# Layer 0 of a two-layer graph network: neighbours summed before the weights are applied, one tile of zeros for two fills, and moved register loads and stores in layer 1

## The chip, the cores and the metric

The kernel runs on one core of a Trainium2 chip. The metric is device microseconds (us) of one execution, taken as the median of several runs. One execution was also recorded by the hardware profiler; all rows below come from that one. Engines are named as in the profile: PE (matrix products; PEld is its weight load), DVE (vector), ACT (scalar and activation functions), POOL, SP (issues most transfers). A small q behind a name (SPq) is the engine's own instruction queue.

## The reference, cut to what matters

Two layers of the same kind, on 3327 tokens of 256 features. Each is a graph step and then a mixture of experts, both added to x:

```python
# layer 0
x = x + relu(adj @ (_layernorm(x) @ W) + b)                      # graph step
xn = _layernorm(x)
gate_scores = xn @ Wg.T + bg                                     # 8 experts, best 2
x = x + sum_e combine[:, e] * (relu(xn @ W1[e].T + b1[e]) @ W2[e].T + b2[e])   # hidden 1024
# layer 1
xn = _layernorm(x)
h2 = tanh(xn @ W_proj + b_proj)
x = x + relu(top700(tanh(adj * adj)) @ (h2 @ W_gcn) + b_gcn)
xn = _layernorm(x)
x = x + xn + sum_e combine[:, e] * (gelu(xn @ w1[e] + b1[e]) @ w2[e] + b2[e])  # hidden 256
```

The layer norm has no learnt scale or shift. `adj` is 3327 x 3327 in float32, with about one entry in 400 set. A row of it keeps its largest 700 entries in layer 1, which changes nothing while no row has more.

## The kernel before

Tokens are padded to 26 tiles of 128 (`NT`). `x` and `s` hold all tiles on the chip, 128 tokens on the partitions and 256 features along a row. The adjacency comes transposed from memory in 13 panels (`NPAN`) of 256 output tokens; a panel is two pieces (`NCHUNK`) of 13 source tiles (`CJ`), 1664 KB each, and lies in a ring of six buffers (`RING`), so three panels fit.

**Layer 0, features (L1021 to L1037).** For the 26 tiles in groups of 2, 2, 4, 4, 6 and 8, DVE works out mean and deviation (`statistics`, L254 to L279, with three Newton steps for the root). PE turns each raw tile by two 128x128 transposes (L304), ACT copies two turned tiles at once (L305), PE multiplies by the weights (`node_features`, L312), and ACT scales the result by the deviation into `s` (L317). The mean is taken out of the weights once, by a product with a tile of 1/256 (L1030, L1033). 32 small matmuls (`WARM`, L144) run on PE ahead of all this.

**Layer 0, panels (`aggregate`, L348 to L367).** For each panel PE sums over the 26 source tiles, for each of its two output tiles in turn: the weights of the array are 128x128 of the adjacency, the moving operand is a row of `s` (L358). DVE adds bias and relu onto `x` (L322, L323), then `after0` normalises the two finished tiles, takes 16 score products (L378, with `gate`, the expert gates spread over all partitions) and ranks them. The tokens of panel p are written to their experts' lists in memory one panel later (`list_tokens`): PE needs the ranks (`rt_both`, L415) for counting them (L464, L465), POOL issues the scatters (L482). ACT counts the set entries of each piece (`count`, L1046, 16 activations a panel) to see that no row exceeds 700; ACT also takes the exponential of the weights (L443), which DVE waits for (L445).

**Fill and gates.** Behind the panel loads `after0(0)` has SP transpose both layers' gates into memory, element by element (L1062, 2048 elements each), has POOL load the first one spread over partitions (L247), and calls `fill`: for each expert's list a tile of zeros with row numbers in one column is made by POOL (L1009, L1010) and stored by SP (L1013), 8 in `after0(0)` and 8 in `after0(1)`. The tiles come from a pool of two.

**Experts.** A step handles one block of up to 256 listed tokens of one expert: `first` (turned block times w1, L865, function on ACT, L872), the transposes of the next block (L853), `second` (L904, bias and weight on DVE, L911, L912, then scatter to `ys`). Blocks are loaded five ahead into the ring by SP: list rows (L820), w1 (L827), b1 (L831), and for some w2 and b2. In layer 1 all of w2 and b2 is on the chip.

**Layer 1, end.** `plan` works out on the chip which blocks exist; a flag says whether the counts are as usual, and both engines branch (L1297). Inside, `know` reads the experts of the last columns into registers of PE and DVE (L789), since those of the first 16 are known numbers. There are 32 steps. From the 17th on, pairs of finished token tiles are read back from `ys` (L968), added to `x` by DVE two steps later (L982), and stored by SP another step later (L1304); the last pairs follow in `finish` (L1266).

Every engine works through its own instruction list in order. The lists are made when the program is built, by priorities and dependencies; an instruction that waits holds up all behind it on its engine, and on SP and POOL the transfers behind it. SP's transfers take eight semaphores in turn, so that one is issued when the transfer eight places before it has landed.

Of the kernel before, what the change touches and what calls it, by code (L numbers as in the profile page):

```python
# [22 lines left out]
P = 128  # L23
NT = 26
# [52 lines left out]

BEGUN, FIRST_TILES, MORE_TILES = 12, 14, 22
WARM = 32
# [11 lines left out]
def gnn_moe_two_layers(  # L91
# [39 lines left out]

    proj_sb = const.tile([P, DC, D], F32, name="proj_sb")
    for t, n in [(0, 2)] + [(t, 4) for t in range(2, NT, 4)]:
        nc.sync.dma_start(out=x[:, t : t + n, :], in_=x_in[:, t : t + n, :])
        if t == 0:
            nc.sync.dma_start(out=proj_sb, in_=g0_w.rearrange("(c p) n -> p c n", p=P))
# [10 lines left out]
    mean = ring[RING - 1][:, 0:P]  # L147
    nc.gpsimd.memset(mean, 1.0 / D)
# [95 lines left out]
    gates = []  # L244

# [6 lines left out]
    g1_bp_sb = plain("g1_bp_sb", g1_bp)  # L252
    g1_wg_sb = by_feature("g1_wg_sb", g1_wg)
# [54 lines left out]
    def node_features(i, lhsT, w_sb, scale=None):  # L308

        ps = psy.tile([P, D], F32, name="ps_s", tag="py")  # L310
        for c in range(DC):
            nc.tensor.matmul(  # L312
                ps, lhsT=lhsT[:, c, :], rhs=w_sb[:, c, :], start=(c == 0), stop=(c == DC - 1)
            )
        if scale is None:
            return nc.scalar.copy(s[:, i, :], ps)
        return nc.scalar.activation(s[:, i, :], ps, AF.Copy, scale=scale)  # L317
# [12 lines left out]
    def piece(pan, k):  # L330
        return ring[(pan * NCHUNK + k) % RING].rearrange("p (c w) -> p c w", w=PW)

    last_piece, output_loads = [], []

    def load_panel(pan, prepare, earlier=()):

        for k in range(NCHUNK):
# [6 lines left out]
    def aggregate(b_sb, prepare, after, loaded=0, count=None):  # L344

        for pan in range(NPAN):
# [4 lines left out]
            if count:  # L351
                count(pan, chunks)
# [14 lines left out]
            after(pan)  # L367

# [383 lines left out]
    def experts(xlist, ys, group, fixed, n_hidden, func, w1T, b1, w2T, b2, copy, kept=None):  # L752
# [5 lines left out]
        own_n, all_w2, all_b2 = kept or (EARLY + LATE, None, None)  # L758
# [18 lines left out]
        def expert(t, late, engines):  # L777

            table, col = late[0] if t >= EARLY else early_table, col_of(t)
            if known and t >= EARLY:  # L780
                if col < known[0]:
                    return col % E
                if engines != [SP]:
                    return known[1][col - known[0]]
            return nc.values_load(table[0:1, 0, col : col + 1], engines=engines, min_val=0, max_val=E - 1)

        def know(n, late):

            _, registers = nc.values_load_multi_w_load_instructions(  # L789
                late[0][0:1, 0, n : LATE_PAIRS + fixed], engines=[PE, DVE], min_val=0, max_val=E - 1  # L790
            )
            known[:] = [n, registers]
# [12 lines left out]
        def load_one(late):  # L805
# [21 lines left out]
            nc.sync.dma_start(  # L827
                out=w1, in_=w1T[ds(e, 1), :, :].rearrange("o (c p) h -> p (o c) h", p=P)
            )
            bb1 = view("b1")  # L830
# [89 lines left out]

        always = EARLY + LATE_PAIRS + fixed

        def step(late, end=always, place=None):
# [8 lines left out]
            hT = first(ready.pop(t), w1, bb1, groups_of(t))  # L932
            if t + 1 < min(len(loaded), end):
# [21 lines left out]
        def back_to(old):  # L955
# [8 lines left out]
            state=state, back_to=back_to, know=know, tiers_done=tiers_done(), always=always,  # L964
# [38 lines left out]
    def fill(xlist):  # L1003

        with tc.issue_after(last_feature.ins):
            for e in range(E):
                zeros = blk.tile([P, H // P, SB], F32, name="wide").rearrange("p h b -> p (h b)")
                zeros = zeros[:, 0 : SG * RW].rearrange("p (g d) -> p g d", g=SG)
                nc.gpsimd.memset(zeros, 0.0)  # L1009
                nc.gpsimd.tensor_scalar(  # L1010
                    zeros[:, :, ID], slot, float(AWAY + SPARE + (LATE + e) * SB), None, ALU.add
                )
                nc.sync.dma_start(  # L1013
                    out=xlist[e * NP : e * NP + SB, :].rearrange("(g p) d -> p g d", p=P),
                    in_=zeros,
                )

    deviation = {}  # L1021
    for t0, n0 in [(0, 2), (2, 2), (4, 4), (8, 4), (12, 6), (18, 8)]:
        _, rs = statistics(t0, n0)
        deviation.update((t0 + g, rs[:, g : g + 1]) for g in range(n0))
        for t in range(t0, t0 + n0, 2):
            xT = turned_tiles([x[:, t + g, :] for g in range(2)])
            if t == 0:
                ps = psy.tile([P, D], F32, name="ps_mean", tag="py")
                for c in range(DC):
                    nc.tensor.matmul(  # L1030
                        ps, lhsT=mean, rhs=proj_sb[:, c, :], start=(c == 0), stop=(c == DC - 1)
                    )
                nc.vector.tensor_tensor(  # L1033
                    proj_sb, proj_sb, ps.unsqueeze(1).to_broadcast([P, DC, D]), ALU.subtract
                )
            for g in range(2):
                last_feature = node_features(  # L1037
                    t + g, xT[:, :, ts(g, P)], proj_sb, deviation[t + g]
                )

    def count(pan, chunks):
        with tc.issue_after(last_feature.ins):
            for k, a in enumerate(chunks):
                for i in range(PW // GROUP):
                    sign = work.tile([P, CJ, GROUP], BF16, name="sign", bufs=1)
                    nc.scalar.activation(  # L1046
                        sign, a[:, :, ts(i, GROUP)], AF.Sign, bias=below,
# [446 lines left out]
```

## Time and profile before

| | |
|---|---|
| median of 3 runs | 1244.86 us (1243.46 to 1245.89) |
| profiled execution, its own time | 1245.38 us |
| its span | 1243.6 us |
| instructions | 18251 |
| PE busy | 1202.0 us, 97% of the span |
| DVE / ACT / POOL busy | 698.0 / 522.5 / 280.9 us |
| moved | 241.60 MB, mean 194 GB/s |
| layer 0: first matmul of the panels, last of them | 44.30 us, 344.87 us |
| layer 1: last matmul of the panels | 1094.86 us |
| last matmul of all | 1226.25 us |

The span is what the records cover; 1.8 us of the execution's own time lie around it. In the lists of waits the columns are: engine, the instruction's output tile and line, what released it, then the sum of the idle time in us, how often, and the longest. In a timeline they are: start in us, duration in us, engine, line, operation, output and inputs, shape, count, and in brackets the idle time before it and what ended it. A matmul of float32 on 128x128 with 256 columns shows as two records.

### The profile page before, as it was taken

The numbers are of one execution on the slowest core, as the hardware profiler recorded it, in microseconds if no ns is written. First come the engines' busy times: TensorE is split into PE (matmuls) and PEld (weight loads), VectorE is DVE, ScalarE is ACT, GpSimd is POOL, SyncE is SP. The second block draws the span as 40 slices with busy tenths as digits, with TensorE's granted clock in tenths as the row PEclk, the third lists the DMA queues.
The fourth block names the chain that finished last, engine by engine and source line by source line (L and its number), as shares of the span: only waits on it lengthen the run. The fifth ranks groups of instructions, "written<-read, shape, count | busy, mean of one in ns | idle before, by whom it ended". The sixth has DMA issues, their size and how long they took to land. (4 is left out here: it accounts for less than half of the span.)

```text
span 1243.6 us, 18251 instructions
## 1 busy us (share of the span) xinstructions
PE 1202.0 (97%) x5853; PEld 1040.3 (84%) x5853; DVE 698.0 (56%) x2812; ACT 522.5 (42%) x963; POOL 280.9 (23%) x367
## 2 busy tenths in 40 slices
PE   7999899999999999999999999999999999999993
PEld 6888788888888888888888888888888888877882
DVE  5064967768755111211111166658999998875464
ACT  4785654551022222222232235895555453043331
POOL 2022313112122111111111110002422323254441
PEclk9999899999999999999999999999999999999997
DMA  9568445544266567575757676344554442476697
GB/s 346 169 194 279 158 169 200 179 146 155 98 215 208 181 197 237 178 230 180 232 173 242 209 273 237 110 149 152 192 182 167 166 176 85 122 247 206 200 296 236
DMA packets 119738, 241.60 MB, mean 194 GB/s; under 512 B 21568, under 2 KB 90192, under 8 KB 112592
## 3 DMA queue, kind: packets, MB, share of 16 engines
q1 hardware_dynamic: 107984, 208.23, 50.2%
q0 software_dynamic: 11104, 31.59, 7.0%
q8 instruction: 48, 0.79, 0.3%
q14 instruction: 58, 0.48, 0.1%
q10 hardware_dynamic: 544, 0.52, 0.1%
HBM read 203.99 MB, written 36.33 MB: 193 GB/s over the span
## 5 line engine op out<-in xcount | busy, mean ns | idle before, releaser
L358 PE MATMUL ps_g<-s,ring 128*128 128x256 f32 x2704 | 591.0, 381 | 0.0
L358 PEld LDWEIGHTS ps_g<-s,ring 128*128 128x128 f32 x2704 | 514.2, 191 | 69.2
L865 PE MATMUL ps_h<-xT,ring 128*128 128x256 f32 (+1 forms) x1176 | 250.1, 366 | 2.7 <-DVE xT L856 1.1
L865 PEld LDWEIGHTS ps_h<-xT,ring 128*128 128x128 f32 x1176 | 205.5, 191 | 39.2 <-ACT wide L872 4.8
L872 ACT ACTIVATE wide<-ps_h,ring 128x256 f32<-128x256 f32 (+1 forms) x240 | 110.2, 459 | 286.0 <-PE ps_h L865 285.0
L378 DVE SCALAR_TENSOR_TENSOR rt_product<-xn,gate 128x256 f32<-128x256 f32 x400 | 197.0, 493 | 12.4
L904 PE MATMUL ps_y<-ring,wide 128*128 128x256 f32 x896 | 200.4, 379 | 0.0
L482 POOL DMA_INDIRECT xlist<-xn,rt_idx x104 | 106.3, 1023 | 371.6 <-DVE ln_ve L269 296.0
L904 PEld LDWEIGHTS ps_y<-ring,wide 128*128 128x128 f32 x896 | 167.2, 190 | 20.9
L1046 ACT ACTIVATE sign<-ring,below 128x416 bf16<-128x416 f32 x208 | 133.5, 642 | 71.6 <-DMA ring<-in_adjT 65.5
L482 POOL DMA_INDIRECT ys<-narrow,index x56 | 54.3, 969 | 331.9 <-DVE narrow L912 245.9
L1197 ACT ACTIVATE ring<-ring 128x3328 f32<-128x3328 f32 x22 | 65.4, 2979 | 87.2 <-DVE ring L1196 56.6
L856 DVE COPY xT<-ptb 128x512 f32<-128x512 f32 (+1 forms) x29 | 19.0, 654 | 146.3 <-PE ptb L853 146.3
L911 DVE TENSOR_TENSOR narrow<-ps_y,ring 128x256 f32<-128x256 f32 x56 | 23.8, 424 | 133.7 <-PE ps_y L904 132.2
L322 DVE TENSOR_TENSOR gnn_t<-ps_g,gnn_b_sb 128x256 f32<-128x256 f32 x52 | 21.9, 421 | 119.4 <-PE ps_g L358 106.4
L482 POOL DMA_INDIRECT ys<-wide,index x58 | 57.8, 996 | 61.2 <-DVE wide L912 35.3
L1198 ACT ACTIVATE ring<-ring 128x3328 f32<-128x3328 f32 x22 | 65.4, 2979 | 0.6
L872 ACT ACTIVATE narrow<-ps_h,ring 128x256 f32<-128x256 f32 (+1 forms) x64 | 28.9, 453 | 68.6 <-PE ps_h L865 66.5
L443 ACT ACTIVATE rt_d<-rt_d 128x2 f32<-128x2 f32 x26 | 5.3, 202 | 123.2 <-DVE rt_d L442 123.2
L904 PE MATMUL ps_y<-s,narrow 128*128 128x256 f32 (+1 forms) x200 | 49.0, 386 | 0.1
L266 DVE BATCH_NORM_STATS2 ln_st<-x 128x6 f32<-128x256 f32 x104 | 42.9, 419 | 6.1 <-DMA x<-in_x 5.0
L1196 DVE TENSOR_SCALAR ring<-ring 128x3328 f32<-128x3328 f32 x22 | 41.3, 1882 | 0.0
(212 smaller groups left out, 983.9 us busy)
## 6 DMA issues: line engine op xcount, KB each, us to landing
ring<-in_adjT SPq DMA_DIRECT2D x52, 1664.0 KB, 7.3
ring<-in_f_w1T SPq DMA_DIRECT2D x30, 1024.0 KB, 6.1
ring<-in_f_w2T SPq DMA_DIRECT2D x30, 1024.0 KB, 7.8
ring<-xlist SPq DMA_DIRECT2D x52, 258.0 KB, 3.0
ring<-in_f_w SPq DMA_DIRECT2D x36, 256.0 KB, 3.6
ring<-ys SPq DMA_DIRECT2D x14, 512.0 KB, 5.2
ring<-in_f_b SPq DMA_DIRECT2D x34, 128.0 KB, 8.0
xlist<-wide SPq DMA_DIRECT2D x16, 258.0 KB, 6.4
```

The costliest lines, as they stand in the source:

```text
L266: nc.vector.bn_stats(out=st, in_=x[:, t0 + g, :])
L358: nc.tensor.matmul(ps[it], lhsT=chunks[k][:, c, ts(it, P)], rhs=s[:, j, :], start=(j == 0), stop=(j == NT - 1),)
L378: nc.vector.scalar_tensor_tensor(product, xn[:, g, 0, 0:D], 1.0, gate[:, e, :], ALU.mult, ALU.mult, accum_out=sc[:, g, e : e + 1],)
L482: d = nc.gpsimd.indirect_dma_start(out=a[:, :], out_offset=bass.IndirectOffsetOnAxis(ap=index, axis=0), in_=rows_, in_offset=None,)
L865: nc.tensor.matmul(ps, lhsT=w1[:, c, ts(hc, P)], rhs=xT[:, c, :], start=(c == 0), stop=(c == DC - 1),)
L872: nc.scalar.activation(hT[:, hc, :], ps, func, bias=bb1[:, hc : hc + 1])
L904: last_product[:] = [nc.tensor.matmul(ps, lhsT=hT[:, hc, ts(g, P)], rhs=w2[:, hc, :], start=(hc == 0), stop=(hc == hc_n - 1),)]
L911: nc.vector.tensor_tensor(y[:, g, :], ps, bb2, ALU.add)
L1046: nc.scalar.activation(sign, a[:, :, ts(i, GROUP)], AF.Sign, bias=below, accum_out=positive[:, pan, i, k : k + 1],)
L1196: nc.vector.tensor_scalar(a, a, 0.0, None, ALU.max)
L1197: nc.scalar.activation(a, a, AF.Square)
L1198: nc.scalar.activation(a, a, AF.Tanh)
```

## The change

- **Layer 0 sums tokens, not features.** `s` now holds the normalised tokens, written by DVE (`layernorm(..., xn=s...)`); the transposes, the mean product and the deviation scaling are gone. A panel sums adj times tokens with the roles on PE exchanged (weights: 128 features of `s`; moving operand: the 256 columns of the piece), which gives the sum already turned. ACT copies it (`g`), and `finish` multiplies it by the weights: four matmuls, then bias and relu, and `after0`. `finish` of a panel runs 6 source tiles (`BEHIND`) into the next panel.
- **Start.** SP loads x and the first pieces of panels 0 and 1 in slices, in turn; PE goes through the first 13 source tiles for both panels at once. The first gate is transposed right behind them and the second behind the loads of panel 1. `WARM` is 54.
- **Fill.** One tile of zeros and one of row numbers serve all 16 stores of both lists; the row numbers are stored by themselves, so there are 32 transfers, all issued ahead of panel 3's load.
- **Between the layers' steps.** `finish` of the last panel runs between the two halves of block 0 of the experts; block 0 of each layer is turned on PE before the last panel instead of behind it.
- **Layer 1, end.** All of b1 is loaded once, at the start; steps with a known expert use it and don't load their own. `know` no longer reads registers at the branch; `know_rest` does, behind step 22. The stores of finished tiles go from SP to ACT. The read-back of pair 8 and later starts one step later.

```diff
-WARM = 32
+BEHIND = 5
+WARM = 54
...
-    for t, n in [(0, 2)] + [(t, 4) for t in range(2, NT, 4)]:
+    for t, n in [(0, 2), (2, 2), (4, 4), (8, CJ - 8), (CJ, NT - CJ)]:
         nc.sync.dma_start(out=x[:, t : t + n, :], in_=x_in[:, t : t + n, :])
-        if t == 0:
-            nc.sync.dma_start(out=proj_sb, in_=g0_w.rearrange("(c p) n -> p c n", p=P))
+        if t < CJ:
+            for pan in range(2):
+                nc.sync.dma_start(
+                    out=piece(pan, 0)[:, t : t + n, :], in_=adjT[pan, 0, :, t : t + n, :]
+                )
+    turn_gate(f0_wgT)
+    nc.sync.dma_start(out=proj_sb, in_=g0_w.rearrange("(c p) n -> p c n", p=P))
...
+    f1_b1_sb = plain("f1_b1_sb", f1_b1)
...
+    def aggregate_first(b_sb, w_sb, begin, count, after):
+        sums, waiting = {}, []
+        def start(pan):
+            sums[pan] = [psy.tile([P, PW], F32, name="ps_g", tag="py") for _ in range(DC)]
+        def add(pan, j):
+            for c in range(DC):
+                nc.tensor.matmul(
+                    sums[pan][c],
+                    lhsT=s[:, j, ts(c, P)],
+                    rhs=piece(pan, j // CJ)[:, j % CJ, :],
+                    start=(j == 0),
+                    stop=(j == NT - 1),
+                )
+        def finish():
+            pan, g = waiting.pop()
+            for it in range(PW // P):
+                ps = psh.tile([P, D], F32, name="ps_o", tag="ph")
+                for c in range(DC):
+                    nc.tensor.matmul(
+                        ps, lhsT=g[:, c, ts(it, P)], rhs=w_sb[:, c, :], start=(c == 0),
+                        stop=(c == DC - 1),
+                    )
+                add_relu(x[:, pan * (PW // P) + it, :], ps, b_sb)
+            after(pan)
+        def rest(pan, first):
+            for j in range(first, NT):
+                add(pan, j)
+                if waiting and j == first + BEHIND:
+                    finish()
+            g = work.tile([P, DC, PW], F32, name="xnT", bufs=2)
+            for c in range(DC):
+                nc.scalar.copy(g[:, c, :], sums[pan][c])
+            waiting.append((pan, g))
+        loaded = RING // NCHUNK
+        for pan in range(loaded):
+            load_panel(pan, lambda pan, k, a: None, begun=1 if pan < 2 else 0)
+            if pan == 1:
+                turn_gate(f1_rT)
+        begin()
+        for pan in range(2):
+            start(pan)
+        for j in range(CJ):
+            for pan in range(2):
+                add(pan, j)
+        for pan in range(NPAN):
+            if pan > 1:
+                start(pan)
+            if loaded < min(pan + RING // NCHUNK, NPAN):
+                load_panel(loaded, lambda pan, k, a: None)
+                loaded += 1
+            count(pan)
+            rest(pan, CJ if pan < 2 else 0)
+        return finish
...
+            if isinstance(e, int):
+                loaded.append((d, xb, w1, all_b1[:, e, :], None, None))
+                return
             bb1 = view("b1")
...
+            for xlist in lists:
+                for e in range(E):
+                    first = xlist[e * NP : e * NP + SB, :].rearrange("(g p) d -> p g d", p=P)
+                    nc.sync.dma_start(out=first[:, :, 0:ID], in_=zeros)
+                    with nc.allow_non_contiguous_dma("two elements of a partition"):
+                        nc.sync.dma_start(
+                            out=first[:, :, ID : ID + 1], in_=rows_f[:, e, :].unsqueeze(2)
+                        )
+    for t0, n0 in [(0, 2), (2, 2), (4, 4), (8, 4), (12, 6), (18, 8)]:
+        layernorm(t0, n0, xn=s[:, t0 : t0 + n0, :].unsqueeze(2))
...
+        if pan == NPAN - 2:
+            layer0.turn_first()
+    finish_last = aggregate_first(
+        gnn_b_sb, proj_sb, lambda: fill(xlist0, xlist1), count, after0
+    )
-    layer0.step(None)
+    layer0.step(None, between=finish_last)
...
-            layer1.know(2 * E, late1)
+            layer1.know(2 * E)
...
-                    nc.sync.dma_start(out=rows_of(out, *tiles), in_=x[:, tiles[0] : sum(tiles), :])
+                    nc.scalar.dma_start(out=rows_of(out, *tiles), in_=x[:, tiles[0] : sum(tiles), :])
                 added.clear()
+                if at == EARLY + 2 * E - 2:
+                    layer1.know_rest(late1)
...
-                if waiting and at > waiting[0][1] + 1:
+                if waiting and at > waiting[0][1] + (1 if k < FIRST_TILES // 2 else 2):
```

## The prediction

> **What bounds the kernel now.** I read the busy times first, then what PE waits for, then PE's timeline at the places of those waits, then the engines that released them.
>
> ```profile
> PE 1202.0 (97%) x5853; PEld 1040.3 (84%) x5853; DVE 698.0 (56%) x2812; ACT 522.5 (42%) x963; POOL 280.9 (23%) x367
> ```
>
> PE bounds it: 41.6 us of the span are not PE's, and 17.3 of those lie behind its last matmul. So a gain is either PE work that goes or one of these waits:
>
> ```profile
> PE ps_s L312 <- ACT xnT L305: 5.2, 6, 3.3
> PE ptb L853 <- DMA ring<-xlist: 4.5, 3, 2.4
> PE pr L464 <- DVE rt_both L415: 3.7, 1, 3.7
> PE ps_h L865 <- issue: 2.9, 1, 2.9
> PE pt L304 <- DMA x<-in_x: 2.0, 1, 2.0
> PE ps_h L865 <- DVE xT L856: 1.1, 1, 1.1
> ```
>
> All but the second and fourth are in layer 0. PE's timeline there:
>
> ```profile
> 37.58 3.72 PE L312 MATMUL ps_s<-proj_sb,xnT 128*128 128x256 f32 x16 [0.29 <-ACT xnT L305]
> 41.13 0.60 PE L304 MATMUL pt<-ident,x 128*128 128x128 f32 x4
> 44.30 45.06 PE L358 MATMUL ps_g<-s,ring 128*128 128x256 f32 x208
> 89.29 22.69 PE L358 MATMUL ps_g<-s,ring 128*128 128x256 f32 x104
> 138.34 0.19 PE L464 MATMUL pr<-rt_both,before 128*128 128x8 bf16 x1 [3.72 <-DVE rt_both L415]
> 138.56 21.70 PE L358 MATMUL ps_g<-s,ring 128*128 128x256 f32 x87
> ```
>
> The features are made one after another until 44.30, and nothing of the panels runs before. A panel takes 104 records in 22.5 us, 0.2167 each. After the wait of 3.72 us at 138.34, 87 records take 21.7 us instead of 18.8: the wait cost 2.9 us more, in a lower clock. What caused it stands in SP's and DVE's timelines:
>
> ```profile
> 18.54 23.69 SPq L1062 DMA_DIRECT2D gate<-in_f_rT  x1
> 42.34 27.74 SPq L1013 DMA_DIRECT2D xlist<-wide  x5
> 121.62 0.17 DVE L445 TENSOR_SCALAR xn<-rt_d 128x2 f32<-128x2 f32 x1 [17.20 <-ACT rt_d L443]
> ```
>
> SP sits on the second gate until 42.2 and then on fills that wait for POOL's two tiles (39.5 us in all); panel loads come late between them, ACT's counting waits for those pieces, the exponential is behind the counting, and DVE behind the exponential.
>
> **The start.** Gone: 52 transposes, the mean product and 104 feature records. Added: four matmuls a panel, 13 x 4 x 2 records x 0.2165 (16 in about 3.5 from start to start) = 22.5 us, at L312's rate, since the shape is the same. The panels' own 2704/2 records stay, the roles exchanged at the same shape, so I keep 0.2167. PE's first panel matmul now needs the first normalised tile and three slices. DVE's first statistics start at 3.76; its dependent steps come 0.2 us apart, nine of them behind the seed, with the next pair's statistics (0.8) between and 0.35 for the normalisation (0.73 for two at L288): 8.5 us. The earliest is the end of 54 warm-up matmuls, 1.06 + 54 x 0.105 (3.37 for 32) = 6.8; the latest 12.3, where before the next pair's root was done. So 44.3 - 22.5 - 8.5 = **13.3 gained** (9.5 to 15).
>
> **Three waits take its place.** (a) 26 normalisations, 9.1 us, join DVE's 18.6. PE takes 1.73 us a tile while it does two panels (four matmuls). Tiles 4 to 7 come behind the second pair (12.6): the rest of their statistics (1.3), twelve dependent steps of 0.2, 0.35: tile 4 is ready at 16.6, PE there at 15.4. Tile 12 stands behind 14 statistics and its root, from 24.3 on; ten such with roots between took 5.0 (17.2 to 22.2), so 7: ready at 31.2, PE there at 30.5. **1.9 lost** (0 to 5). (b) The second piece of panel 0 is behind 6.8 MB of x and slices and the first gate. 6.0 MB had moved by 20 us (302 GB/s) and 423 GB/s later; with 0.55 MB of POOL's that is 23.3 us. The gate's elements: 988 small packets went by between 48 and 52 us, so 2048 take up to 8; I take 6. With weights and piece (1.9 MB) it lands at 33.8; PE wants it at 8.5 + 22.5 + 1.9 = 32.9. **1 lost** (0 to 6). (c) Panel 0's ranks are wanted right behind `finish` of panel 1. From panel 0's first finished tile to there PE has the rest of panel 1 and six tiles of panel 2, 14.1 us. DVE needs 3.2 for two tiles' bias, relu and statistics and 12.8 from there to the ranks (68.5 to 81.3 before), 16.0. **1.9 lost** (0 to 4).
>
> **Panel 3 and the fills.** 32 transfers are issued ahead of panel 3's load. They move 4.2 MB, at the 300 GB/s of such rows 14 us, and 4096 single elements, at 250 to 330 in a us 12 to 16. They start behind panel 2, at about 50, and end at about 78; the piece takes 4 more. PE wants it at 33.9 + 22.5 + 22.5 + 2 x 1.73 + 1.9 = 84.3. POOL's part is done by 12 us, so SP no longer waits for it. The margin of 2.3 is less than these rates are sure: **1 lost** (0 to 7). Then panels are loaded a whole panel ahead, and the old wait with its clock goes: **6.6 gained** (0 to 6.6).
>
> At one rule the Trainium skill speaks against this part. The row: the first 20 us, mostly packets of 4 KB and less, moved 302 GB/s, by which the 5.0 MB of slices take 17 us. "DMA: Bandwidth & Descriptors", section Bandwidth, wants transfers of 1 MiB or more and gives 341 GB/s for 1 MB and 138 for 64 KB; the slices have 256 to 640 KB. By an estimate midway, 240, they would take 21, wait (b) would grow by 4 and the sum be 4 less. I go by the row.
>
> **Block 0.** Turned ahead of the last panel, it no longer waits for its copy: 1.1 gained; `finish` between its halves needs the two buffers that the steps use, 0 to 1.5 lost, I take 0.4. **0.7 gained.** In layer 1 the same saves the 0.67 before L865 at 1096.28: **0.8 gained**, with ACT free since 1089.
>
> **The branch in layer 1.** PE idles 2.88 at 1130.97, and the next eight records take 3.65 instead of 1.89. The flag is there at 1130.0. The 16 register moves are one part, the branch and its code the other; no row parts them. All of it would be 4.6, none 0, and moved behind step 22 the load itself can cost 0 to 1 (three such loads at 1098.3 cost 0.2). I take **2 gained**, nearest to the middle as no row decides.
>
> **The last stretch.** PE waits 5.2 us for list rows there:
>
> ```profile
> 1203.80:1226.30 22.50, 17.16 (x93) 13.71 (x92) 10.71 (x36) 7.00 (x19) 8.74 (x9) 0.92 0.96 289
> ```
>
> The columns are the span of the stretch, busy times of PE, PEld, DVE, ACT, POOL, the clock, the DMA share and GB/s. The transfers are busy for 96% of it, so fewer waits on SP only let some go sooner. SP's stores go, with up to 5.4 us of waits for DVE, and read-backs come a step later, when the scatters have landed (11.5 us of SP's waits). Against it: the stores now stand in ACT's list and wait for DVE's additions, which waited 16.5 us for read-backs; behind them stand the copies for PE. Bounds -4 to 5; **1 gained**, near nothing because of the 96%. b1's ten absent loads are off PE's path, with SP's waits as cover.
>
> **Sum.** 13.3 - 1.9 - 1 - 1.9 - 1 + 6.6 + 0.7 + 0.8 + 2 + 1 = 18.6. From the profiled execution's 1245.38: 1226.8; that one is 0.5 above the median of the runs, 1244.86, so 1226.3 by it. I say **1227**.
>
> **Rivals.**
> 1. *The start starves.* Second pieces and panel 3 come late: (b) 6 and the fills 5 instead of 1 each. Each idle time over 3 us would bring the 2.9 of clock seen at 138.56; with one of them, 9 + 2.9, less the 1.9 of (c) that then hides: 1227 + 10 = 1237. For it: DMA shows 9 in nearly all slices to 40 us. Against: those bytes were loaded before too, by 40.
> 2. *ACT's stores hold PE.* Nine additions waited 16.5 us for read-backs. PE has a product of 1.9 us beside each, so half of a wait is charged, 8; SP's earlier read-backs save 3 of it: 1227 + 5 = 1232. For: share 0.88 in slices 38 and 39. Against: psum has four buffers, and read-backs are later.
> 3. *The waits don't come and the end flows.* (a) to (c) and fills at nothing (5.8), 3 more at the end: 1218.
> 4. *Slower: the fills stall panel 3.* If element stores go one behind another's landing (the first old fill held SP for 9.3 us), at 3 us each the 32 end at 50 + 96 = 146 instead of 78 and the piece at 150; PE stands from 84.3, 66 us instead of 1: about 1292. It decides from 1.5 us a transfer (49 us for all 32): there the 18.6 are gone. Against: eight may be under way at once.
>
> That the change does not do what it says (PE still waiting for all tiles) is excluded by the built order: its first panel matmul stands right behind the warm-up.
>
> **Chances.** Forecast 0.62, rival 1 0.16, rival 2 0.09, rival 3 0.08, rival 4 0.05. 0.2% (2.5 us) is about what a measurement of this kernel can tell from no change. Faster 0.93, same 0.02 (rival 4 with a smaller price), slower 0.05. The range takes in the forecast and rivals 1 to 3 and leaves their far ends: 1217 to 1239.
>
> **What would show it.** First panel matmul near 8.5 us; last one of layer 0, with the 12 finishes, near 329; PE waits at tiles 4 and 12, at the second piece, at the first ranks, each under 3 us; no wait near 138; at the branch under 2 us of idle PE. Wrong if SP's fills end after 85 us, or if PE waits for ACT's xT copies behind stores from step 18 on.

## The result and the profile after

The change made the kernel slightly **slower**: 1245.18 us median of 20 runs (1243.35 to 1248.73), beside 1242.26 for the kernel before (20 runs, 1238.32 to 1247.17); ratio 1.0028, 95% interval 1.0017 to 1.0040. A gain of 18.6 us was forecast; 2.9 were lost. The profiled execution took 1244.48 us, with a span of 1242.8.

The first row is the page's busy times, the rest the list of what PE waits for, both of the changed kernel:

```profile
PE 1194.6 (96%) x5819; PEld 1032.8 (83%) x5819; DVE 705.7 (57%) x2837; ACT 508.7 (41%) x950; POOL 278.9 (22%) x338
```

```profile
PE ps_g L390 <- DVE s L304: 5.7, 2, 4.4
PE ps_g L390 <- DMA ring<-in_adjT: 4.0, 1, 4.0
PE ptb L932 <- ACT narrow L951: 3.8, 2, 2.8
PE ps_h L944 <- ACT xT L935: 3.6, 2, 2.0
PE ps_o L403 <- ACT xnT L417: 3.6, 3, 2.4
PE pr L536 <- DVE rt_both L487: 1.7, 1, 1.7
```

PE works 7.4 us less and waits more. The old waits are gone (feature copies, the 3.72 at 138, the idle time at the branch); new ones stand at the start, at panel 3, at the copies of a panel's sum (L417) and, in the last steps, at ACT. PE's timeline of the changed kernel at these places:

```profile
11.31 23.69 PE L390 MATMUL ps_g<-ring,s 128*128 128x256 f32 x96 [4.44 <-DVE s L304]
36.21 1.99 PE L390 MATMUL ps_g<-ring,s 128*128 128x256 f32 x8 [1.21 <-DVE s L304]
93.67 7.93 PE L390 MATMUL ps_g<-ring,s 128*128 128x256 f32 x24 [4.04 <-DMA ring<-in_adjT]
103.96 1.99 PE L403 MATMUL ps_o<-proj_sb,xnT 128*128 128x256 f32 x8 [2.36 <-ACT xnT L417]
1129.52 1.91 PE L944 MATMUL ps_h<-xT_arms,ring 128*128 128x256 f32 x8
```

The 96 records from 11.31 on would take 20.8 us at 0.2167 each and take 23.69; the 24 from 93.67 on would take 5.2 and take 7.93. Both follow four microseconds of idle PE; the granted clock was 0.50 from 11.31 to 16.7 and from 93.67 to 98.6, then 1.00:

```profile
11.31:16.70 5.39, 5.39 (x13) 4.33 (x14) 4.77 (x26) 0.00 (x0) 0.00 (x0) 0.50 1.03 399
93.67:98.60 4.93, 4.92 (x12) 3.94 (x13) 0.00 (x0) 4.69 (x13) 0.00 (x0) 0.50 1.01 429
```

(The third column from the right is the granted clock.) After idle times of 1.21 and 2.36 there is no such loss in this profile. The Trainium skill ("TensorE: Matmul & The Clock Gate", Part 1) says that the array falls to half clock after an idle window of about 3.4 us and comes back after about as long at work. The fall to half agrees with this trace; the way back took longer here, 5.4 and 4.9 us. Nor does the length of the idle time alone decide: a run below (the second list's fill) lost time after 2.21 us and none after 2.66.

SP's timeline of the changed kernel shows why the panels come late, ACT's why the copies do:

```profile
13.42 11.81 SPq L155 DMA_DIRECT2D proj_sb<-in_g_w  x1
26.87 17.77 SPq L351 DMA_DIRECT2D ring<-in_adjT  x2
82.10 7.93 SPq L351 DMA_DIRECT2D ring<-in_adjT  x6
```

```profile
93.71 0.64 ACT L1121 ACTIVATE sign<-ring,below 128x416 bf16<-128x416 f32 x1 [19.66 <-DMA ring<-in_adjT]
103.56 0.62 ACT L417 COPY xnT<-ps_g 128x256 f32<-128x256 f32 x2
```

SP stood 11.8 us behind the first gate's elements and 17.8 behind the second's, then stored fills until 81.7; only then was panel 3's load issued. On ACT the two copies of panel 2's sum, ready when PE had done that panel, at 89.6, ran at 103.56: in ACT's built order they stand behind thirteen of the sixteen counting instructions of panel **3**, and these waited for panel 3's load.

The last steps, one chain through three timelines of the changed kernel (DVE, ACT's queue, ACT, PE):

```profile
1189.44 0.69 DVE L1067 TENSOR_TENSOR x<-x,ring 128x512 f32<-128x512 f32 x1 [3.71 <-DMA ring<-ys]
1190.89 0.38 ACTq L1376 DMA_DIRECT2D out_x<-x  x1
1191.37 0.58 ACT L935 COPY xT<-ptb 128x512 f32<-128x512 f32 x1 [3.00 <-DVE wide L990]
1192.01 1.99 PE L944 MATMUL ps_h<-xT,ring 128*128 128x256 f32 x8 [1.98 <-ACT xT L935]
```

DVE waits for a read-back, ACT for DVE's addition before it can issue the store, the copy for PE's next block stands behind that store, and PE waits. Its last matmul ends at 1221.3 instead of 1226.25, yet the span is 0.8 shorter only: from the last matmul to the end it is 21.5 us instead of 17.3.

### The profile page after: what moved, and what is told of

It is laid out like the page before. It is cut to its first block, busy times and chain, and to the rows that moved or that the text cites. A ratio compares the mean times of both kernels' runs of the same rounds, so it can differ in the third digit from the quotient of the medians.

```text
span 1242.8 us, 18142 instructions
## 1 busy us (share of the span) xinstructions
PE 1194.6 (96%) x5819; PEld 1032.8 (83%) x5819; DVE 705.7 (57%) x2837; ACT 508.7 (41%) x950; POOL 278.9 (22%) x338
## 5 line engine op out<-in xcount | busy, mean ns | idle before, releaser
L390 PE MATMUL ps_g<-ring,s 128*128 128x256 f32 x1352 | 301.1, 385 | 10.4 <-DVE s L304 5.7
L390 PEld LDWEIGHTS ps_g<-ring,s 128*128 128x128 f32 x1352 | 259.3, 193 | 47.5 <-DVE s L304 6.2
L367 PE MATMUL ps_g<-s,ring 128*128 128x256 f32 x1352 | 294.2, 380 | 0.0
L367 PEld LDWEIGHTS ps_g<-s,ring 128*128 128x128 f32 x1352 | 256.0, 190 | 34.4
L336 DVE TENSOR_TENSOR gnn_t<-ps_o,gnn_b_sb 128x256 f32<-128x256 f32 x26 | 11.0, 424 | 80.2 <-PE ps_o L403 80.2
```

Source lines behind the costliest of these rows:

```text
L367: nc.tensor.matmul(ps[it], lhsT=chunks[k][:, c, ts(it, P)], rhs=s[:, j, :], start=(j == 0), stop=(j == NT - 1),)
L390: nc.tensor.matmul(sums[pan][c], lhsT=s[:, j, ts(c, P)], rhs=piece(pan, j // CJ)[:, j % CJ, :], start=(j == 0), stop=(j == NT - 1),)
```

## The experiments

The runs came in groups, each on one chip beside its own runs of the kernel before. Medians of the kernel before were 1242.26 (the result above), 1238.33 (first four runs below), 1250.32, 1247.91 and 1248.38; so ratios are compared, and positions in profiles of one group. "End of layer 0" is the start of the first expert matmul (ps_h) of layer 0, "end of layer 1's panels" the same of layer 1.

### First group: the start, the gates, the fills, the stores

**96 warm-up matmuls**

```diff
-WARM = 54
+WARM = 96
```

> The changed kernel with 96 warm-up matmuls instead of 54; they end near 11.1 us (1.07 + 96 x 0.105), so PE's idle 4.44 us before its first panel matmul at 11.31 goes. Both theories expect the clock of the first 96 panel records back (20.8 us instead of 23.69). Theory A (panel 3 is bound by SP's queue, which issues its load at 82.1 whatever PE does): PE arrives earlier at tile 12 and at panel 3 and waits there longer, by 2.9 in all; panel 3 still resumes at 93.7 and the time stays within 0.5 us of the changed kernel's 1245.2. Theory B (PE's losses add up): the 2.9 us arrive at the end, 1242.3.

Ratio 1.0006 (0.9994 to 1.0017). They ended at 9.03, for the warm-up speeds up (96 took 7.96 us, 54 had taken 5.79); 2.12 us idle were left, and 96 records took 21.34 instead of 23.69. But the idle time at tile 12 grew to 3.62, and the 84 records behind it took 20.08 instead of 18.4: what the start gave, the wait for x took, with a clock loss of its own. Layer 0 ended at 338.17, 3.0 sooner than in the run with the stores on SP below (same layer 0, 341.19), because ACT's copies held PE for 2.03 there instead of 4.84; PE reached them at 95.4 in both. So what the start gave was lost at another wait, theory A's mechanism, at tile 12 rather than at panel 3. The time is nearer to theory B's figure (2.7 us below the changed kernel's 1.0028), but by the shorter wait for ACT, not by the start.

**Both gates later**

```diff
-    turn_gate(f0_wgT)
     nc.sync.dma_start(out=proj_sb, ...)
...
             if pan == 1:
-                turn_gate(f1_rT)
+                turn_gate(f0_wgT)
...
                 loaded += 1
+                if pan == 1:
+                    turn_gate(f1_rT)
```

> The changed kernel with the two element-wise gate transposes moved on SP: the first from behind the last slice of x to behind the second piece of panel 1, the second from there to behind the load of panel 3. Theory A (the elements hold SP and what stands behind them: SP stood 11.8 us behind the first gate and 17.8 behind the second): second pieces and panel 2 are issued by 20 us instead of 27 and 45, the fills end near 60 instead of 82, panel 3's load is issued near 62 and PE no longer waits 4.04 us for it, nor runs its 24 records at the lower clock (2.7), nor waits for ACT behind the late counting (2.4 + 1.1): last panel matmul of layer 0 near 334.5 instead of 344.7, time 1235. Theory B (the bytes, not the elements, are late): the last slice of x still lands at 29.4, panel 3's load is issued after 75 and the time moves less than 3 us from 1245.2.

Ratio 0.9974 (0.9958 to 0.9990); layer 0 ended at 336.93. The windows from 20 to 35 us, first of the run with the stores on SP (the changed kernel's start, same group), then of this one; the last two columns are DMA share and GB/s:

```profile
20.00:35.00 15.00, 14.29 (x67) 12.23 (x65) 10.73 (x62) 7.16 (x17) 0.78 (x2) 1.00 0.76 177
```

```profile
20.00:35.00 15.00, 15.00 (x71) 13.22 (x70) 14.28 (x80) 11.66 (x32) 0.00 (x0) 1.00 0.94 332
```

The elements had cost nearly half the rate; the waits at tile 12 are gone. 4.3 us of the 10 came: fills still ended at 69, panel 3's load was issued at 69.94, and PE still waited 1.50 and 3.09 us for ACT's copies. Theory A in kind, less than half in size.

**The second list's fill behind panel 3's load**

```diff
-        gnn_b_sb, proj_sb, lambda: fill(xlist0, xlist1), count, after0
+        gnn_b_sb, proj_sb, lambda later=False: fill(xlist1 if later else xlist0), count, after0
...
                 loaded += 1
+                if pan == 1:
+                    begin(True)
```

> The changed kernel with the fill of the second list (16 of the 32 transfers, from a second tile of zeros) moved on SP behind the load of panel 3. Theory A (the fills ahead of panel 3's load make it late; SP was at them from 44.8 to 81.7): its load is issued near 63 us, the idle time of 4.04 at 93.67 with its clock (2.7) and the waits for ACT behind it (2.4 + 1.1) go, last panel matmul of layer 0 near 335, time 1235. Theory B (the fill is not what is late; panel 3's load waits for the slowness of the queues in that stretch): PE still waits over 2 us for panel 3, and the time stays above 1242.

Ratio 1.0020 (1.0008 to 1.0032); layer 0 ended at 339.83, 1.4 sooner than unmended in this group. The load was issued at 68.1 and PE no longer waited for panel 3, but 2.21 and 2.66 us for ACT's copies stayed:

```profile
96.31 3.07 PE L403 MATMUL ps_o<-proj_sb,xnT 128*128 128x256 f32 x8 [2.21 <-ACT xnT L417]
125.25 1.99 PE L403 MATMUL ps_o<-proj_sb,xnT 128*128 128x256 f32 x8 [2.66 <-ACT xnT L417]
```

The first cost 1.1 us more in its eight records and 0.6 in the next 104, at a granted clock of 0.50 from 97.5 to 100; behind the longer one the clock stayed at 1.00. The late load was not what mattered most; theory A failed.

**Stores of finished tiles on SP**

```diff
-                    nc.scalar.dma_start(out=rows_of(out, *tiles), ...)
+                    nc.sync.dma_start(out=rows_of(out, *tiles), ...)
```

> The changed kernel with the stores of finished tiles in the last steps of layer 1 issued by SP again instead of ACT. Theory A (on ACT's list they wait for DVE's additions, and hold the copies and functions behind them): PE's waits for ACT from 1185 us on (1.64, 1.98, 2.78 and 1.24 = 7.6 us) go, but SP's own waits for DVE (5.4 us before the change) come back and hold list rows; 2 to 5 us are left, time 1240 to 1243. Theory B (the end is set by read-backs and transfers, not by PE): last matmul moves, the end by less than 1 us, 1244 to 1246.

Ratio 0.9991 (0.9977 to 1.0004). PE's waits for ACT from 1183 on are gone, 2.8 us of waits for list rows and weights are there instead, and from the branch block to the last matmul PE needs 89.0 us; 91.6 to 92.0 in the three others of the group. Theory A: the run with the split fill, whose layer 0 ended 1.4 us sooner, took 2.8 us more. In the same profile panel 3 cost 0.95 us and ACT's copies 4.84: the unmended layer 0 divides its loss differently from one execution to the next.

### Second group: layer 1's edits, and layer 0 mended

**The kernel before, registers read behind step 22**

```diff
-            layer1.know(2 * E, late1)
+            layer1.know(2 * E)
...
+                if at == EARLY + 2 * E - 2:
+                    layer1.know_rest(late1)
```

> The kernel before, with one edit: the registers of PE and DVE for the last experts are read behind step 22 instead of at the branch. Theory A (PE's 2.88 us of idle time at the branch and the 1.76 of clock behind it come from those register reads, and the end follows PE): PE comes through the branch without idle time, 4.6 us are gained there and 3 to 4.6 at the end: 0.3% faster than the kernel before, and so the changed kernel's loss lies wholly elsewhere. Theory B (the last stretch is bound by its transfers, busy for 96%): the 4.6 us are gained at the branch and lost again before the last matmul, time within 1.2 us of the kernel before. Beside it: if layer 0's idle time of 3.72 us at 138 differs here from that of the first profile, that stall is not the same in every execution.

Ratio 0.9995 (0.9977 to 1.0012). At the branch of this run:

```profile
1132.70 2.95 PE L869 MATMUL ps_h<-xT_arms,ring 128*128 128x256 f32 x8 [2.91 <-ACT xT_arms L860]
```

The idle time is as long as before; only what it waits for is another: ACT's copy, ahead of which ACT itself had stood idle for 3.84 us and DVE for 3.27, released by nothing that the profile names. No gain shows, and the 0.3% of theory A lies outside the interval. And the side question had the larger answer: there is **no wait near 138**, and layer 0 ended at 339.65 instead of 346.71.

**The last steps as before (SP stores, no later read-back)**

```diff
-                    nc.scalar.dma_start(out=rows_of(out, *tiles), ...)
+                    nc.sync.dma_start(out=rows_of(out, *tiles), ...)
...
-                if waiting and at > waiting[0][1] + (1 if k < FIRST_TILES // 2 else 2):
+                if waiting and at > waiting[0][1] + 1:
```

> The changed kernel with both edits of its last steps undone: stores of finished tiles on SP, and every pair read back two steps after its wait begins (the later read-back of pair 8 on is gone). Theory A (only the stores on ACT cost; the later read-backs are worth something): slower than the variant with the stores alone on SP (0.9991 of the kernel before) by 1 to 3 us, 1.000 to 1.002. Theory B (later read-backs only push the end out): faster than that variant by 1 to 3 us, 0.997.

Ratio 1.0035 (1.0020 to 1.0049). It doesn't compare with the run it was set against: layer 0, the same in both, ended 4.0 us later here (345.18; panel 3 alone cost 4.48). It decides nothing on the later read-backs.

**Layer 0's transfers in another order**

```diff
-WARM = 54
+WARM = 80
...
+    nc.sync.dma_start(out=x[:, 0:4, :], in_=x_in[:, 0:4, :])
...
-    turn_gate(f0_wgT)
...
             if pan == 1:
-                turn_gate(f1_rT)
+                turn_gate(f0_wgT)
...
+            if pan == 3:
+                turn_gate(f1_rT)
+            if pan == 5:
+                begin(True)
```

> The changed kernel, its last steps untouched, with the order of SP's transfers in layer 0 mended: the first four tiles of x ahead of the slices of the adjacency, 80 warm-up matmuls, the first gate behind the second piece of panel 1, the second gate behind panel 3 and the second list's fill behind panel 5. Theory A (the 14.8 us forecast for layer 0 are there once nothing stands in SP's queue ahead of its panels): first panel matmul near 9 us, no idle time over 1 us behind 80 us, last panel matmul of layer 0 near 330 us instead of 344.7 and 336.9 (gates moved alone), 1228 to 1231 where the kernel before takes 1238.3 (0.993). Theory B (the start is bound by bytes and by DVE's normalisation): the last panel matmul stays above 335 and the time above 0.996.

Ratio 0.9980 (0.9965 to 0.9995). The first panel matmul ran at 9.74, layer 0 ended at 335.48: 6 to 10 us sooner than the unmended layer 0 in its five profiles (341.19 to 345.18, the last from this group), not the 15 expected. Behind 80 us one wait over 2 us was left: 4.20 us at 94.08, again for ACT's copies (L418 there). Theory B's bounds were met, but not for its reason: this wait is neither for bytes nor for the normalisation.

**The same, with the stores on SP**

The edit is the one of the first group's stores, on top of the order above.

> The same mended layer 0, and the stores of finished tiles on SP instead of ACT. Theory A (the two losses add up; stores on ACT cost 0.3 to 0.4%): 3 to 5 us less than with the mended layer 0 alone, 0.989 to 0.990 of the kernel before. Theory B (they don't add, the end being bound by read-backs): within 1.2 us of it.

Ratio 0.9959 (0.9943 to 0.9975): 2.6 us less, between the two theories. The two intervals overlap, but the sign is that of the first group.

### Third group: the kernel before again, ACT's order, all together, layer 0 alone

**The kernel before, unchanged**

> The kernel before, unchanged, for a second profile. Theory A (the stall of 3.72 us at 138 and the clock behind it, 7 us in all, belong to the profiled execution and not to the kernel; the same layer 0 ended 7.1 us sooner, at 339.65 instead of 346.71, when only layer 1 was edited): no idle time over 1 us between 50 and 340 us, first matmul of the experts of layer 0 near 339.7. Theory B (the stall is the rule): it is there again with 3 to 4 us, near 346.

One execution, 1247.91 us, as its group's median of the kernel before. PE, then DVE of the kernel before, second profile:

```profile
41.03 45.06 PE L358 MATMUL ps_g<-s,ring 128*128 128x256 f32 x208
132.22 0.18 PE L464 MATMUL pr<-rt_both,before 128*128 128x8 bf16 x1 [0.86 <-DVE rt_both L415]
```

```profile
115.53 0.17 DVE L445 TENSOR_SCALAR xn<-rt_d 128x2 f32<-128x2 f32 x1 [14.43 <-ACT rt_d L443]
```

The same chain as in the first profile (SP, ACT's counting, exponential, DVE) is some 6 us earlier, and PE, which arrives at the same place, waits 0.86 instead of 3.72, with no loss of clock. The panels began at 41.03 instead of 44.30. Layer 0 ended at 337.90. Theory A: the first profile showed a slow layer 0 of a kernel whose layer 0 was 7 and 9 us shorter in the two others. The early start of the panels is not the rule, though: in the profile with the registers read behind step 22, which has the same layer 0, they began at 43.91.

**ACT's counting behind its copies**

```diff
-                nc.scalar.copy(g[:, c, :], sums[pan][c])
+                copied[:] = [nc.scalar.copy(g[:, c, :], sums[pan][c])]
...
-            count(pan)
+            with behind(copied):
+                count(pan)
```

> The changed kernel with one edit: ACT's counting of a panel's pieces is issued behind ACT's copies of the panel before. In the changed kernel's built order the copies of panel 2 stand behind 12 counting instructions of panel 3, whose pieces land late. Theory A (PE's waits for ACT's copies at 103.96 and 129.66 come from that order): both waits go, 2.4 + 1.1 and some clock, 3 to 5 us gained against the changed kernel (1.0028 of the kernel before), so 0.999 to 1.0005; panel 3's own wait for its load stays. Theory B (the copies only wait because panel 3 itself ends late): the waits go but panel 3 or 4 waits longer instead, within 1.2 us of the changed kernel.

(The copies stand behind thirteen counting instructions, not twelve.)

Ratio 0.9976 (0.9963 to 0.9990): some 6 us off the changed kernel, more than theory A's 3 to 5. Layer 0 ended at 333.05; in the run with layer 0 alone below, on the same chip and with only ACT's order different in layer 0, at 341.76. ACT, then PE of that other run (unmended order):

```profile
90.04 0.64 ACT L1121 ACTIVATE sign<-ring,below 128x416 bf16<-128x416 f32 x1 [16.13 <-DMA ring<-in_adjT]
99.88 0.62 ACT L417 COPY xnT<-ps_g 128x256 f32<-128x256 f32 x2
```

```profile
100.28 3.78 PE L403 MATMUL ps_o<-proj_sb,xnT 128*128 128x256 f32 x8 [4.83 <-ACT xnT L417]
```

and ACT, then PE of this one:

```profile
88.80 0.80 ACT L417 COPY xnT<-ps_g 128x256 f32<-128x256 f32 x2 [0.58 <-PE ps_g L390]
```

```profile
94.21 1.89 PE L403 MATMUL ps_o<-proj_sb,xnT 128*128 128x256 f32 x8
```

SP issued panel 3's load at the same time in both (79.63 and 79.13). With the copies ahead of the counting, the finish runs without a wait and at full clock; nothing else had to be moved.

**All mendings**

The transfers in the other order, the counting behind the copies, and the stores on SP.

> All the mendings together: four tiles of x first, 80 warm-up matmuls, gates and the second list's fill later, counting behind the copies, stores of finished tiles on SP. Theory A (ACT's order was the cause of the 4.2 us of idle PE at 94 that the mended layer 0 still had): no wait over 2 us behind 80 us, first matmul of the experts of layer 0 near 329.5 to 331, 4 to 6 us less than without the pinned counting (0.9959), 0.991 to 0.9925 of the kernel before. Theory B (another transfer takes its place): still a wait over 3 us near 94, 0.995 or more.

Ratio 0.9904 (0.9885 to 0.9922), 1236.79 us: faster than both kernels. PE's timeline holds three waits in layer 0; the first two:

```profile
9.74 21.00 PE L391 MATMUL ps_g<-ring,s 128*128 128x256 f32 x96 [2.08 <-DVE s L305]
32.34 18.40 PE L391 MATMUL ps_g<-ring,s 128*128 128x256 f32 x84 [1.60 <-DVE s L305]
```

The third is the one for the first ranks, 1.66. Layer 0 ended at 328.63. Theory A, and a little more than it expected.

**Layer 0 alone**

```diff
-        aggregate(gnn_b_sb, filter_chunk, panels1(layer1, True), loaded=ahead)
+        aggregate(gnn_b_sb, filter_chunk, panels1(layer1), loaded=ahead)
...
             layer1.know(2 * E)
+            layer1.know_rest(late1)
...
```

and the two edits of the last steps as above.

> The changed layer 0 with layer 1 as in the kernel before: registers read at the branch, block 0 turned behind the last panel, stores on SP, read-backs without the later step (b1 stays preloaded). Theory A (the start and layer 0 lose against the usual execution of the kernel before, and layer 1 gains): 4 to 8 us slower, 1.003 to 1.0065. Theory B (layer 0 is neutral, as the two first profiles say, and the last steps lose): within 0.2% of the kernel before.

Ratio 1.0022 (1.0009 to 1.0035), below theory A's range and above B's bound by a hair. Layer 0 alone loses about what the whole change loses (1.0028, and 1.0023 in the last group): layer 1's edits together gave nothing that these intervals show.

### Fourth group: one edit at a time on the mended kernel

Each of the first three takes back one edit whose diff stands above.

**Stores on ACT again**

> The kernel with all mendings (0.9904 of the kernel before), with one taken back: stores of finished tiles on ACT again, as the change has them. Theory A (stores on ACT's list wait for DVE's additions and hold PE's copies; 2.6 us where only SP's order in layer 0 was mended): 2 to 5 us slower than with all mendings, 0.992 to 0.9945. Theory B (the end is set by read-backs): within 1.2 us of it.

Ratio 0.9919 (0.9901 to 0.9938). Waits for ACT of 2.41 and 2.83 us in the last steps are back; from the last matmul to the end 21.2 us, 19.0 with all mendings, whose own profile has one wait for ACT there, of 3.17, with no store in ACT's list ahead of it. The time is about 1.9 us longer, at the lower edge of theory A, and the intervals overlap.

**No later read-back**

> The kernel with all mendings and no later step for the read-back of pair 8 and later. Theory A (read-backs a step sooner wait at SP for the scatters, and hold list rows behind them): 1 to 3 us slower than with all mendings, 0.991 to 0.993. Theory B (sooner read-backs bring the last additions and the end sooner): 1 to 2 us faster, 0.989.

Ratio 0.9892 (0.9870 to 0.9915), the lowest time of all, 1234.30 us. The interval holds the 0.9904 with all mendings: the later read-backs give nothing that shows, and may cost.

**Registers at the branch again**

> The kernel with all mendings, the registers for the last experts read at the branch again. Theory A (2.5 to 2.9 us of idle PE at the branch come back, and the end follows PE): 2 to 4.6 us slower than with all mendings, 0.992 to 0.994. Theory B (the time saved at the branch is lost again in the last steps, as in the kernel before, where the same edit gave 0.9995): within 1.2 us, 0.990 to 0.9915.

Ratio 0.9919 (0.9900 to 0.9938). The idle time at the branch is back (2.66 us). As with the stores, the difference to 0.9904 is about 1.9 us, and the intervals overlap.

**The changed kernel, unchanged**

> The changed kernel, unchanged, beside the three others and the kernel before on the same chip. Theory A (ACT's order and SP's queue hold layer 0 in every execution, and the stall of the kernel before at 138 is not in every one): again waits of PE for panel 3 or for ACT's copies between 90 and 130 us, 4 us or more in all, layer 0's first expert matmul between 341 and 345, ratio 1.001 to 1.004. Theory B (the changed kernel's first profile was an unlucky one too): no such waits, layer 0 ended near 335, ratio under 1.000.

Ratio 1.0023 (1.0011 to 1.0036), 1251.09 us, where the mended kernel with the stores still on ACT took 1239.06 in the same group: 12.0 us for the order on SP and ACT in layer 0. Panel 3 cost 0.69 and ACT's copies 4.83 this time, layer 0 ended at 341.25. Theory A.

## Why the prediction was wrong

The steps of layer 0, forecast beside what two profiles of one chip show, the kernel before again and layer 0 alone (third group), in us:

| step | forecast | measured |
|---|---|---|
| the start | +13.3 | 41.03 - 22.5 - 11.71 = +6.8 |
| clock behind the start | not in the sum | 104 records 25.21 instead of 22.69: -2.5 |
| (a) normalised tiles | -1.9 | 0 |
| (b) second piece of panel 0 | -1 | -1.9 |
| (c) first ranks | -1.9 | -1.7 |
| fills and panel 3 | -1 | 0.50 and 24 records 5.45 instead of 5.2: -0.8 |
| old wait at 138 with its clock | +6.6 | +0.9 |
| ACT's copies of a panel's sum | not in the sum | 4.83, then 1.8 and 0.8 of clock: -7.4 |
| block 0 | +0.7 | taken as forecast |
| sum | +14.8 | -5.9 |

The end of layer 1's panels moved from 1088.82 to 1094.73, which is -5.9. The medians say less (2.7): the profiled execution of layer 0 alone was 3.2 above the median of its own runs. And the panels of the kernel before began as early as 41.03 only in this profile; against the 43.91 and 44.30 of the two others the start gained 9.7 and 10.1.

Term (b) is told by two rows of the run with layer 0 alone, ACT's and PE's:

```profile
38.76 0.64 ACT L1121 ACTIVATE sign<-ring,below 128x416 bf16<-128x416 f32 x1 [11.79 <-DMA ring<-in_adjT]
38.81 16.64 PE L390 MATMUL ps_g<-ring,s 128*128 128x256 f32 x76 [1.90 <-DVE s L304]
```

ACT's counting and PE begin together, when the second piece of panel 0 has landed: at 38.8 instead of the 33.8 forecast. It cost no more than 1.90 because PE came at 36.9 instead of 32.9. (The profile puts PE's wait down to a tile of `s` that PE needs later.)

- **The step that failed most is one that isn't there.** The change puts a copy by ACT between a panel's sum and its weights, and the prediction charged nothing for where that copy stands in ACT's list. It spoke of ACT's counting as the cause of the old wait, and then let the new copies run freely beside the same counting. The built order told it: copies of panel 2 behind counting of panel 3. One pinned order gave 8.7 us of layer 0's end, and some 6 us of the time.
- **The old wait (6.6) was a gain over one execution.** Its range went down to nothing, but the sum took the upper end. The sum was made against the first profile's own time, whose total (1245.38) lay close to the median shown; its layer 0 did not. Of three profiles of this layer 0 it was the only one with that stall.
- **The start**: the first tile was ready at 11.3, not 8.5. DVE's steps stand in the order that the prediction gives, but the next pair's statistics wait for x (3.21 us of idle DVE at 9.69), whose slice stands behind adjacency slices. With four tiles of x first (and 80 warm-up matmuls) it was 9.74. The idle time of 4.4 to 4.9 us ahead of it then cost 2.5 to 2.9 more in a lower clock, which the prediction charged to a rival only.
- **Fills and gates** were sized too low: SP ended the fills at 81.7, inside the bound of 85 that the prediction named, but without room. On the question of rates the row was right: 295 GB/s moved in the first 20 us of the changed kernel, and 178 from there to 35, behind the elements. The estimate of 240 for slices of these sizes, which the prediction worked out from the figures of the Trainium skill ("DMA: Bandwidth & Descriptors", section Bandwidth), was not borne out by them.
- **Last steps and branch**: rival 2's mechanism was there, stores on ACT holding PE: 1.9 to 2.6 us by the pairs of the second group and of the mended kernel, whose intervals overlap in both. The branch gave 0 to 2, the forecast's 2 being the upper end; how much is not settled, nor whether read-backs a step later cost anything.
- Rival 1 named late pieces and the lost clock, but priced them at 10 where they came to be part of 21. Rival 4's way to the slower side (fills stalling panel 3 by 66 us) did not happen; panel 3 cost 0.5 to 4.5 in five executions of the unmended layer 0.

The forecast's own place for the end of layer 1's panels, 1096.28 - 14.8 - 0.8 = 1080.7, is where the mended kernel has it: 1080.81. That the two fit to 0.1 is luck: the mended kernel begins its panels 1.2 us later than forecast, waits 0.5 less, has another order of transfers and ran on another chip. But the arithmetic of the panels held; what failed is the account of the queues, and the baseline.

## What to carry to other kernels

When a change puts a small step of another engine between two pieces of work of the busy engine, look up where that step stands in the built list of its engine, and what the instructions ahead of it wait for; the order that was fixed when the program was built can put it behind a panel that isn't there yet. Before a stall is booked as a gain, see whether it is there in a second profile, or don't book the upper end of its range. Put element-wise transfers behind the loads that the busy engine needs, not among them.

## What the runs showed of the hardware

The same kernel's stretch from layer 1's first expert matmul to the branch took 34.1 us in five profiles (the changed kernel's first and the first group), 37.6 in the first of the kernel before, and 40 to 46 us in all twelve of the later groups, changed or not. A row of the changed kernel's second profile, fourth group:

```profile
1119.33 2.92 PE L983 MATMUL ps_y<-s,narrow 128*128 x6 [3.16 <-issue]
```

PE waits there for nothing that the profile shows, as it does several times in that stretch; the records do not name the cause, and no run tried it. The stretch is long in both kernels and varies from profile to profile (41.4 to 46.4 within the third group), so only medians beside the same group's kernel before are compared; a few us between two single profiles behind layer 1's panels say nothing. Each group ran on a chip of its own, so whether the chip makes the difference stays open too. Its 6 to 12 us are as much as any step of this change did.
